# Local attention in a two-stage transformer kernel: exponentials transposed in 32x32 blocks on VectorE, mixing over 32 keys on four row groups, inverse norms on GpSimd

## The chip, the core and the metric

The kernel runs on one core of a Trainium2 chip. The metric is the device time of one execution in microseconds (us). Below, PE is TensorE (PEld its weight loads), DVE is VectorE, ACT is ScalarE, POOL is GpSimd, SP issues DMAs.

## The reference

The input is 16 sequences of 256 tokens of 128 numbers, all fp32. Three blocks run first (a linear attention, a mixture of experts, a causal attention with softmax feature maps), each with a residual and a layer norm. The fourth block has six layers, and the change lies in them. A layer, for each sequence:

```python
q, k, v = split(shift_tokens(x) @ Wqkv[i])      # 16 heads of 64
q = l2norm(q) * q_scale;  k = l2norm(k) * k_scale
q, k = rotary(q, scale), rotary(k, 1 / scale)
# windows of 32 queries; each sees its own 32 keys and the 32 before them
sim  = einsum('bhwie,bhwje->bhwij', q, k2) * 8.0   # 32 x 64 per window and head
attn = softmax(where(mask, -big, sim))
x = einsum('bhwij,bhwje->bhwie', attn, v2) @ Wo[i] + x
x = feed_forward(shift_tokens(x)) + x            # norm, 128 -> 2 x 341, gelu gate, 341 -> 128
```

A last layer norm ends the program.

## The kernel before, in words

Everything stays in fp32. The tokens of a unit (two sequences) lie in SBUF with the 128 features on the partitions (`xs`, with 32 zero columns ahead of a sequence). The program has two plans: one for the first three blocks, one for the six layers. A plan is a list of steps (`step(engine, work, function, after, takes, uses, rank, ...)`); `Plan.run` (line 87) walks them in a modelled time with the declared `work` of each in us, and on each engine issues the ready step of lowest rank whose buffers are free. The issued order is fixed when the program is built. Ranks are the number of the sequence tile plus entries of two tables, the dictionary passed to `Plan` (line 1013) and `due` (line 1028). Buffers come from `slots` (line 992): `pair` are the four PSUM tiles of 128x1024 (two banks each, all of PSUM), the others lie in SBUF.

A sequence is worked on in two tiles `t` of 128 tokens:

- `projections` (line 1059): queries and keys of 16 heads into a pair (PE, line 1071); the squares (ACT, line 1092) and their sums over a head (DVE, line 1098, into `ss`); the two halves of the rotation (DVE, lines 1078 and 1085), added on POOL (line 1095).
- `rotations` (line 1133): `norms` turns the 64 sums of a sequence into inverse norms by an integer first guess and three Newton steps (`inv_norm`, DVE, lines 1046 to 1057); POOL scales (line 1141), PE transposes (line 1145), ACT copies out (line 1151).
- `windows` (line 1180): for mixing, tokens must lie on the partitions, as a window's 64 keys, once in each half of 128 partitions. ACT spreads the tokens (line 1187), PE does 8 transposes (line 1196), ACT copies 1024 columns out (line 1202).
- `attention` (line 1213), for each tile: scores in four calls (PE, line 1228, 64 rows x 32 columns of the array, two heads and four windows side by side); mask and maximum (DVE, 1236, 1250); difference (POOL, 1253); exponential (ACT, 1257); sum and reciprocal (DVE, 1261, 1262); division (POOL, 1265). Then the exponentials `e` (queries on partitions) are turned by 8 transposes (PE, line 1269) and copied to `eT` (ACT, line 1310). Mixing (PE, line 1280) is two calls of four matmuls: for a window of 32 queries and one head of each two, 64 rows (keys) x 128 features, over 256 columns (8 heads x 32 queries). Each call fills one pair, and ACT copies it to `zT` (line 1289). Values are not projected: the product of the value and the output weights (`wvo`, made once a layer by `join`) is applied behind.
- `output` (line 1333): 16 accumulated matmuls over 256 tokens (PE, line 1340); added into `xs` (DVE, line 1349).
- `feed_forward` (line 1355) for each unit, with its gelu on ACT and its `root` on POOL (lines 1381 and 221).

A matmul of fp32 is recorded as two passes, a transpose as one.

Of the kernel before, what the change touches and what calls it, by code (L numbers as in the profile page):

```python
# [9 lines left out]
F32 = mybir.dt.float32  # L10
# [6 lines left out]
P = 128  # L17
NSEQ = 16
SEQ = 256
# [44 lines left out]
class Plan:  # L64
# [22 lines left out]
    def run(self):  # L87
# [15 lines left out]
        while left:  # L103
            moved = True
            while moved:
                moved = False
                for eng, heap in ready.items():
                    if at[eng] > now or not heap:
                        continue
                    back, got = [], None  # L110
                    while heap and len(back) < 64:
                        item = heapq.heappop(heap)
                        s = item[2]
                        if s.table and opened and s.table not in opened:
                            back.append(item)
                            continue
                        if s.count > 32 and self._dense(s, now, past, events):
                            back.append(item)
                            continue
                        kinds = [b.kind for b in s.takes]  # L120
                        if all(self._fits(kinds, k) for k in set(kinds)):
                            got = s
                            break
                        back.append(item)
                    for item in back:
                        heapq.heappush(heap, item)
# [66 lines left out]
def tile_kernel(ctx: ExitStack, tc: tile.TileContext, a: dict, out: bass.AP):  # L193
# [787 lines left out]
    with ExitStack() as st:  # L981
# [6 lines left out]
        def several(pl, n, shape, name):  # L988
# [4 lines left out]
            "pair": several(pp, 4, [P, 1024], "pp"),  # L993
            "kT": several(cd, 2, [P, 8, WIN + SEQ], "d_kT"),
            "qT": several(cd, 3, [P, 8, P], "d_qT"),
            "xw": several(cd, 2, [P, TPS * NB, P], "d_xw"),
            "sq": several(cd, 2, hs, "d_sq"),
            "t1": several(cd, 5, hs, "d_t1"),
            "ss": several(cd, 3, [P, 2, 2, HEADS, 2], "d_ss"),
            "t2": several(cd, 2, hs, "d_t2"),  # L1000
            "e": several(cd, 2, [P, 8, 2, 2 * WIN], "d_e"),
            "eT": several(cd, 2, [P, 8, P], "d_eT"),
            "zT": several(cd, 2, [P, SEQ // QB, HEADS, QB], "d_zT"),
            "xc": several(cd, 1, [P, TPU, P], "f_xc"),
# [5 lines left out]
        for ss in slots["ss"]:  # L1010

            pool.memset(ss, 1e-24)
        plan = Plan(slots, {
            "projections.product": -3,
            "feed_forward.turn": 1.5,
            "attention.mix": -1.5,
            "attention.divide": -0.5,
            "output.product": 2,
            "attention.below": 5,
            "projections.first": -0.5,  # L1020
            "projections.squares": 0.5,
            "projections.second": -1,
            "final.turn_back": -3,
            "windows.turn": -1,
            "rotations.norms": 3,
        })

        due = {
# [14 lines left out]
        magic = cd.tile([P, NN], I32, name="d_magic")  # L1043
        pool.memset(magic, 1597463007)

        def inv_norm(ss):

            x, y, t = (sd.tile([P, NN], F32, name=f"d_n{k}", bufs=2) for k in "xyt")
            dve.tensor_reduce(x, ss.rearrange("p t g h b -> p (t g h) b"), AX.X, ALU.max)
            dve.scalar_tensor_tensor(  # L1050
                y.bitcast(I32), x.bitcast(I32), -0.5, magic, ALU.mult, ALU.add
            )
            for _ in range(3):
                dve.scalar_tensor_tensor(t, y, 1.0, y, ALU.mult, ALU.mult)
                dve.scalar_tensor_tensor(t, t, -0.5, x, ALU.mult, ALU.mult)
                dve.scalar_tensor_tensor(y, t, 1.5, y, ALU.add, ALU.mult)  # L1056
            return y

        def projections(q, t):
# [35 lines left out]
                pool.tensor_tensor(t1.t, t1.t, t2.t, ALU.add)  # L1095

            def squares(qk, sq):
                dve.tensor_reduce(q.ss.t[:, t, qk, :, 0], sq.t, AX.X, ALU.add)  # L1098
# [34 lines left out]
        def rotations(q):  # L1133


            def norms():
                q.rn = inv_norm(q.ss.t)

            def scale(t, qk, t1):
                k = (2 * t + qk) * HEADS  # L1140
# [11 lines left out]
                    dst.t[:, :, off : off + P], pz.t.rearrange("p (c n) -> p c n", n=P)  # L1152
                )

            nm = step("dve", 4.4, norms, q.reds, [], [q.ss], q.rank + due["norms"])
            q.kT = Buf("kT")
            for t in range(TPS):
                turned(q, t, nm, scale, turn, put)
# [21 lines left out]
        def windows(q):  # L1180

            pz, rank = Buf("pair"), q.rank

            def spread():
                x = q.x
                src = bass.AP(x.tensor, x.offset, [x.ap[0], [WIN, TPS * NB], [0, 2], [1, 2 * WIN]])
                act.copy(
                    xd.t.rearrange("p h d -> p (h d)").rearrange(
                        "p (b a k) -> p b a k", a=2, k=2 * WIN
                    ),  # L1190
                    src,
                )

            def turn():
                for b in range(TPS * NB):
                    pe.transpose(
                        pz.t[:, b * P : (b + 1) * P],
                        xd.t.rearrange("p h d -> p (h d)")[:, b * P : (b + 1) * P], ident,
                    )

            def put():
                act.copy(q.xw.t.rearrange("p b d -> p (b d)"), pz.t)  # L1202

            xd, q.xw = Buf("sq"), Buf("xw")
            begun = every[q.n - 1].soft[0] if q.n else None
            dp = step("act", 0.96, spread, [*q.ready, begun], [xd, q.xw, pz], [], rank)
            tn = step("pe", 1.02, turn, [dp], [], [xd, pz], rank + due["windows"], count=16)
            q.spread = step(
                "act", 0.91,
                put, [tn], [], [pz, q.xw], rank,  # L1210
            )

        def attention(q, t):

# [49 lines left out]
            def divide():  # L1264
                pool.tensor_tensor(each(), each(), bc(o.z, es, 2), ALU.mult)  # L1265

            def turn(pz):
                for c in range(8):
                    pe.transpose(  # L1269
                        pz.t[:, c * P : (c + 1) * P],  # L1270
                        e.t[:, c, :, :].rearrange("p a k -> p (a k)"), ident,
                    )

            def mix(g, pz):

                for j in range(2):
                    b = 2 * g + j
                    for par in range(2):
                        r = slice(par * DH, (par + 1) * DH)
                        pe.matmul(  # L1280
                            pz.t[:, par * 512 : (par + 1) * 512].rearrange(
                                "p (c n) -> p c n", n=QB
                            )[:, :, j * WIN : (j + 1) * WIN],
                            lhsT=q.xw.t[r, t * NB + b, :],
                            rhs=eT.t[r, :, b * WIN : (b + 1) * WIN], start=True, stop=True,
                        )

            def put(g, pz):
                act.copy(q.zT.t[:, 2 * t + g, :, :].rearrange("p h n -> p (h n)"), pz.t)  # L1289

            sc = []
            for g in range(4):
# [14 lines left out]
            pz = Buf("pair")  # L1307

            def put_e():
                act.copy(eT.t.rearrange("p c n -> p (c n)"), pz.t)  # L1310

            te = step(
                "pe", 1.03, partial(turn, pz), [dv], [pz], [e], rank + due["turn"], count=16
            )
            pe_ = step(
                "act", 0.91,
                put_e, [te], [eT], [pz], rank,
            )
            if t == 0:
                q.zT = Buf("zT")  # L1320
            for g in range(2):
                pz2 = Buf("pair")
                new = [q.zT] if t == 0 and g == 0 else []
                mx = step(
                    "pe", 1.06, partial(mix, g, pz2), [pe_, q.spread, *q.mixed[:1]], [pz2, *new],
                    [eT, q.xw] + ([] if new else [q.zT]), rank + due["mix"], count=16,
                )
                q.mixed.append(mx)
                q.outs.append(
                    step("act", 0.91, partial(put, g, pz2), [mx], [], [pz2, q.zT], rank)  # L1330
                )

        def output(q):

            pr = Buf("pair")

            def product():

                for h in range(HEADS):
                    pe.matmul(  # L1340
                        pr.t[:, :SEQ], lhsT=q.w["vo"][:, h, :], rhs=q.zT.t[:, :, h, :],
                        start=(h == 0), stop=(h == HEADS - 1),
                    )
# [331 lines left out]
```

## Time and profile before

| | |
|---|---|
| median of 3 runs | 4375.44 us (4375.12 to 4377.77) |
| the profiled execution | 4371.72 us |
| its span, first to last instruction | 4369.9 us |
| mean granted PE clock | 0.989 |
| instructions | 106,120 |
| DMA | 37.13 MB, mean 8 GB/s |

The page gives for each engine its busy time, then a row of 40 slices of the span (a digit is the busy share in tenths, PEclk the clock that PE was granted), then groups of instructions: line, engine, operation, destination and sources by the program's names, shapes, count, then busy us and mean ns of one, then idle time ahead of them and who ended it. The end of a matmul is modelled, so that times of PE calls are read better from start to start.

### The profile page before, as it was taken

What the parts mean: (1) busy time and instruction counts of PE and PEld (TensorE: products, weight loads), DVE (VectorE), ACT (ScalarE), POOL (GpSimd) and SP (SyncE); (2) the same over time, 40 slices, a digit from 0 to 9 for tenths busy, and PEclk for the clock granted to TensorE, in tenths of its full rate; (3) what the DMA queues carried; (4) which work ended last, traced back from release to release, by engine and by line L of the source; (5) the groups of instructions that cost most, each with busy time, mean ns of one, the idle gap of its engine ahead of it and who ended that gap; (6) DMA issues with size and microseconds to landing.
All of it is one profiled execution on the core that took longest, in us unless ns stands there. A gap on an engine that the chain in (4) does not pass through costs nothing. (4 is left out here: it accounts for less than half of the span.)

```text
span 4369.9 us, 106120 instructions
## 1 busy us (share of the span) xinstructions
PE 4191.8 (96%) x45648; PEld 2978.9 (68%) x45648; DVE 3633.8 (83%) x6064; ACT 2674.8 (61%) x3514; POOL 2978.6 (68%) x1717
## 2 busy tenths in 40 slices
PE   8999999998699999999999999999999999999998
PEld 6777877877466666666666666666666666666666
DVE  6888888877788888878888888888888878888895
ACT  6766767664466566566656656666665665665654
POOL 2655545555787777767777778777777777777773
PEclk9999999999899999999999999999999999999999
DMA  3000000000000000000000000000000000000000
GB/s 88 4 6 6 3 4 1 4 3 3 20 2 11 2 13 2 7 11 2 13 2 6 11 2 13 2 7 11 2 12 2 7 11 2 2 2 6 6 14 18
DMA packets 30834, 37.13 MB, mean 8 GB/s; under 512 B 5407, under 2 KB 24349, under 8 KB 29597
## 3 DMA queue, kind: packets, MB, share of 16 engines
q1 hardware_dynamic: 30364, 30.35, 2.3%
q8 instruction: 359, 5.88, 0.6%
q14 instruction: 111, 0.90, 0.1%
HBM read 26.15 MB, written 4.19 MB: 7 GB/s over the span
## 5 line engine op out<-in xcount | busy, mean ns | idle before, releaser
L1095 POOL TENSOR_TENSOR d_t<-d_t,d_t 128x1024 f32<-128x1024 f32 x384 | 906.3, 2366 | 301.7 <-DVE d_t L1078 230.7
L1141 POOL TENSOR_TENSOR d_t<-d_t,d_ny 128x1024 f32<-128x1024 f32 x384 | 718.8, 1902 | 242.3 <-DVE d_ny L1056 242.3
L1071 PE MATMUL pp<-d_wqkv,xs 128*128 128x512 f32 x1536 | 736.7, 605 | 6.5 <-ACT d_sq L1092 1.6
L1340 PE MATMUL pp<-d_zT,d_wvo 128*128 128x256 f32 x3072 | 687.5, 382 | 1.2 <-DVE d_t L1078 0.5
L1340 PEld LDWEIGHTS pp<-d_zT,d_wvo 128*128 128x128 f32 x3072 | 575.9, 190 | 85.0 <-ACT d_xw L1202 1.3
L1092 ACT ACTIVATE d_sq<-pp 128x1024 f32<-128x1024 f32 x384 | 393.4, 1024 | 313.8 <-PE pp L1071 174.4
L1085 DVE TENSOR_TENSOR d_t<-pp,d_tab 128x1024 f32<-128x1024 f32 x384 | 466.3, 1215 | 135.4 <-ACT d_sq L1092 94.5
L1265 POOL TENSOR_TENSOR d_e<-d_e,d_z 128x1024 f32<-128x1024 f32 x192 | 363.5, 1902 | 229.6 <-DVE d_z L1262 228.3
L1289 ACT COPY d_zT<-pp 128x1024 f32<-128x1024 f32 x384 | 384.1, 1016 | 192.6 <-PE pp L1280 190.3
L1078 DVE TENSOR_TENSOR d_t<-pp,d_tab 128x1024 f32<-128x1024 f32 x384 | 463.7, 1209 | 19.0 <-ACT d_sq L1092 19.0
L1228 PEld LDWEIGHTS pp<-d_kT,d_qT 64*32 64x32 f32 x24576 | 230.2, 106 | 352.9 <-issue 202.1
L1098 DVE TENSOR_REDUCE d_ss<-d_sq 128x16 f32<-128x1024 f32 x384 | 463.3, 1209 | 0.1
L1280 PE MATMUL pp<-d_eT,d_xw 64*128 64x256 f32 x3072 | 425.9, 402 | 21.7 <-DVE d_t L1078 12.7
L1145 PE MATMUL pp<-ident,d_t 128*128 128x128 f32 x3072 | 404.2, 278 | 35.5 <-POOL d_t L1141 24.0
L1071 PEld LDWEIGHTS pp<-d_wqkv,xs 128*128 128x128 f32 x1536 | 271.4, 191 | 241.5 <-issue 217.2
L1145 PEld LDWEIGHTS pp<-ident,d_t 128*128 128x128 f32 x3072 | 344.8, 142 | 104.6 <-issue 56.4
L1257 ACT ACTIVATE d_e<-d_e 128x1024 f32<-128x1024 f32 x192 | 202.8, 1057 | 317.4 <-POOL d_e L1253 312.7
L1228 PE MATMUL pp<-d_kT,d_qT 64*32 64x64 f32 x24576 | 348.7, 223 | 28.7 <-DVE d_t L1078 25.0
L1253 POOL TENSOR_TENSOR d_e<-d_e,d_m 128x1024 f32<-128x1024 f32 x192 | 363.7, 1903 | 16.7 <-DVE d_m L1250 16.7
L848 POOL TENSOR_TENSOR c_e<-c_e,c_sm 128x1024 f32<-128x1024 f32 x128 | 248.7, 1950 | 178.2 <-DVE c_sm L844 121.8
L1280 PEld LDWEIGHTS pp<-d_eT,d_xw 64*128 64x128 f32 x3072 | 270.7, 187 | 104.0 <-ACT d_eT L1310 28.3
L835 POOL TENSOR_TENSOR c_e<-c_mn,c_e 128x512 f32<-128x512 f32 x128 | 139.7, 1091 | 196.3 <-ACT c_e L825 95.7
(187 smaller groups left out, 8083.1 us busy)
## 6 DMA issues: line engine op xcount, KB each, us to landing
d_wqkv<-L_ffn_Wqkv SPq DMA_DIRECT2D x6, 1024.0 KB
d_t<-L_ffn_Wqkv SPq DMA_DIRECT2D x10, 256.0 KB
d_t<-L_ffn_Wo SPq DMA_DIRECT2D x10, 256.0 KB, 3.0
a_xin<-L_attn_x SPq DMA_DIRECT2D x8, 256.0 KB, 2.9
keep<-bc_x SPq DMA_DIRECT2D x8, 256.0 KB, 2.0
d_t<-keep SPq DMA_DIRECT2D x8, 256.0 KB, 3.0
out<-d_t SPq DMA_DIRECT2D x8, 256.0 KB, 2.4
d_w<-L_ffn_W SPq DMA_DIRECT2D x6, 341.0 KB
```

The lines of the kernel that those rows point to most:

```text
L1071: pe.matmul(pj.t[:, hf * 512 : (hf + 1) * 512], lhsT=xj, rhs=q.w["qkv"][:, c : c + 512], start=True, stop=True,)
L1078: dve.tensor_tensor(t1.t, heads(pj.t), bc(q.lay.tab[:, 0, t, cc], hs, 1), ALU.mult)
L1085: dve.tensor_tensor(t2.t.rearrange("p h (x d) -> p h x d", x=2), swapped(pj.t), bc(q.lay.tab[:, 1, t, cc].rearrange("p (x d) -> p x d", x= ...
L1092: act.activation(sq.t, heads(pj.t), AF.Square)
L1095: pool.tensor_tensor(t1.t, t1.t, t2.t, ALU.add)
L1098: dve.tensor_reduce(q.ss.t[:, t, qk, :, 0], sq.t, AX.X, ALU.add)
L1141: pool.tensor_tensor(t1.t, t1.t, bc(q.rn[:, k : k + HEADS], hs, 2), ALU.mult)
L1145: pe.transpose(pz.t[:, c * P : (c + 1) * P], t1.t[:, 2 * c : 2 * c + 2, :].rearrange("p h d -> p (h d)"), ident,)
L1228: pe.matmul(pS.t[b * WIN : (b + 1) * WIN, s0 : s0 + 2 * WIN], lhsT=qT.t[r, c, b * WIN : (b + 1) * WIN], rhs=kT.t[r, c, k0 : k0 + 2 * WIN], ...
L1280: pe.matmul(pz.t[:, par * 512 : (par + 1) * 512].rearrange("p (c n) -> p c n", n=QB)[:, :, j * WIN : (j + 1) * WIN], lhsT=q.xw.t[r, t * NB ...
L1289: act.copy(q.zT.t[:, 2 * t + g, :, :].rearrange("p h n -> p (h n)"), pz.t)
L1340: pe.matmul(pr.t[:, :SEQ], lhsT=q.w["vo"][:, h, :], rhs=q.zT.t[:, :, h, :], start=(h == 0), stop=(h == HEADS - 1),)
```

## The change

It is in the plan's rule and in the layer stage.

1. The exponentials of a tile are transposed by one DVE instruction in blocks of 32x32 (keys by queries, within each 32 partitions) straight from `e` to `eT`. The 8 PE transposes and the ACT copy go.
2. Mixing takes 32 keys at a time: two halves `j` of the 64 keys accumulate in PSUM. A matmul has 32 rows (one block of keys, on the row group of its block of queries), 128 features, 512 columns (16 heads x 32 queries). One call per tile does all 8 and takes two pairs at once. `zT` has blocks of 32 queries.
3. `windows` transposes 128 tokens straight out of `xs`, at offsets of 0 and 32: four transposes, no spreading, 512 columns copied out.
4. `inv_norm` runs on POOL in 14 instructions over 128x64, with the lower bound as an operation of its own in place of an extra slot in `ss`.
5. Both tables of ranks change. In `Plan.run`, a step that needs two buffers of a kind and has only one free keeps that one from steps behind it.

```diff
                         kinds = [b.kind for b in s.takes]
-                        if all(self._fits(kinds, k) for k in set(kinds)):
+                        if all(self._fits(kinds, k) for k in set(kinds)) and not any(k in kept for k in kinds):
                             got = s
                             break
+                        if not kept:
+                            kept = [
+                                k for k in set(kinds)
+                                if kinds.count(k) > 1
+                                and all(self._fits(kinds, m) for m in set(kinds) - {k})
+                            ]
...
-            "xw": several(cd, 2, [P, TPS * NB, P], "d_xw"),
+            "xw": several(cd, 2, [P, 2 * TPS, P], "d_xw"),
-            "ss": several(cd, 3, [P, 2, 2, HEADS, 2], "d_ss"),
+            "ss": several(cd, 3, [P, TPS, 2, HEADS], "d_ss"),
-            "eT": several(cd, 2, [P, 8, P], "d_eT"),
-            "zT": several(cd, 2, [P, SEQ // QB, HEADS, QB], "d_zT"),
+            "eT": several(cd, 2, [P, 2, HEADS, WIN], "d_eT"),
+            "zT": several(cd, 2, [P, TPS * NB, HEADS, WIN], "d_zT"),
...
-            pool.memset(ss, 1e-24)
         plan = Plan(slots, {
-            "projections.product": -3,
+            "projections.product": -6,
...
+        def inv_norm(x):
+            y, t = (sd.tile([P, NN], F32, name=f"d_n{k}", bufs=3) for k in "yt")
+            pool.tensor_scalar(x, x, 1e-24, None, ALU.max)
+            pool.tensor_scalar(
+                y.bitcast(I32), x.bitcast(I32), -0.5, 1597463007.0, ALU.mult, ALU.add
             )
             for _ in range(3):
-                dve.scalar_tensor_tensor(t, y, 1.0, y, ALU.mult, ALU.mult)
-                dve.scalar_tensor_tensor(t, t, -0.5, x, ALU.mult, ALU.mult)
-                dve.scalar_tensor_tensor(y, t, 1.5, y, ALU.add, ALU.mult)
+                pool.tensor_tensor(t, y, y, ALU.mult)
+                pool.tensor_tensor(t, t, x, ALU.mult)
+                pool.tensor_scalar(t, t, -0.5, 1.5, ALU.mult, ALU.add)
+                pool.tensor_tensor(y, y, t, ALU.mult)
             return y
...
-            nm = step("dve", 4.4, norms, q.reds, [], [q.ss], q.rank + due["norms"])
+            nm = step("pool", 2.8, norms, q.reds, [], [q.ss], q.rank + due["norms"])
...
             def turn():
-                for b in range(TPS * NB):
-                    pe.transpose(
-                        pz.t[:, b * P : (b + 1) * P],
-                        xd.t.rearrange("p h d -> p (h d)")[:, b * P : (b + 1) * P], ident,
-                    )
+                for t in range(TPS):
+                    for j in range(2):
+                        n = 2 * t + j
+                        c = t * P + j * WIN
+                        pe.transpose(pz.t[:, n * P : (n + 1) * P], q.x[:, c : c + P], ident)
             def put():
-                act.copy(q.xw.t.rearrange("p b d -> p (b d)"), pz.t)
+                act.copy(q.xw.t.rearrange("p b d -> p (b d)"), pz.t[:, : 2 * TPS * P])
...
-            dp = step("act", 0.96, spread, [*q.ready, begun], [xd, q.xw, pz], [], rank)
-            tn = step("pe", 1.02, turn, [dp], [], [xd, pz], rank + due["windows"], count=16)
+            tn = step("pe", 0.5, turn, [*q.ready, begun], [pz, q.xw], [], rank + due["windows"], count=8)
...
-            def turn(pz):
-                for c in range(8):
-                    pe.transpose(
-                        pz.t[:, c * P : (c + 1) * P],
-                        e.t[:, c, :, :].rearrange("p a k -> p (a k)"), ident,
-                    )
+            def turn():
+                dve.transpose(
+                    eT.t,
+                    e.t.rearrange("p c a (j k) -> p j (c a) k", j=2),
+                )
-            def mix(g, pz):
+            def mix(ps):
                 for j in range(2):
-                    b = 2 * g + j
-                    for par in range(2):
-                        r = slice(par * DH, (par + 1) * DH)
+                    for b in range(NB):
+                        r = slice(b * WIN, (b + 1) * WIN)
                         pe.matmul(
-                            pz.t[:, par * 512 : (par + 1) * 512].rearrange(
-                                "p (c n) -> p c n", n=QB
-                            )[:, :, j * WIN : (j + 1) * WIN],
-                            lhsT=q.xw.t[r, t * NB + b, :],
-                            rhs=eT.t[r, :, b * WIN : (b + 1) * WIN], start=True, stop=True,
+                            ps[b // 2].t[:, (b % 2) * 512 : (b % 2 + 1) * 512],
+                            lhsT=q.xw.t[r, 2 * t + j, :],
+                            rhs=eT.t[r, j, :, :].rearrange("p h n -> p (h n)"),
+                            start=(j == 0), stop=(j == 1),
                         )
...
+            te = step("dve", 1.15, turn, [dv], [eT], [e], rank + due["turn"])
+            ps = [Buf("pair"), Buf("pair")]
+            new = [] if q.mixed else [q.zT]
+            mx = step(
+                "pe", 2.1, partial(mix, ps), [te, q.spread, *q.mixed], [*ps, *new],
+                [eT, q.xw] + ([] if new else [q.zT]), rank + due["mix"], count=32,
+            )
...
-                        pr.t[:, :SEQ], lhsT=q.w["vo"][:, h, :], rhs=q.zT.t[:, :, h, :],
-                        start=(h == 0), stop=(h == HEADS - 1),
+                        pr.t[:, :SEQ], lhsT=q.w["vo"][:, (h % 2) * 8 + h // 2, :],
+                        rhs=q.zT.t[:, :, h, :], start=(h == 0), stop=(h == HEADS - 1),
```

More of the change, by code (lines that the diff above doesn't have):

```diff
@@ L109, in run @@
                         continue
-                    back, got = [], None
+                    back, got, kept = [], None, ()
                     while heap and len(back) < 64:
@@ L1009, in tile_kernel @@
             pool.memset(kT[:, :, 0:WIN], 0.0)
-        for ss in slots["ss"]:
-            pool.memset(ss, 1e-24)
         plan = Plan(slots, {
-            "projections.product": -3,
+            "projections.product": -6,
             "feed_forward.turn": 1.5,
             "attention.mix": -1.5,
-            "attention.divide": -0.5,
-            "output.product": 2,
+            "attention.divide": -1.5,
+            "output.product": 4,
             "attention.below": 5,
-            "projections.first": -0.5,
+            "projections.first": -4.5,
             "projections.squares": 0.5,
             "projections.second": -1,
-            "final.turn_back": -3,
+            "final.turn_back": -2,
             "windows.turn": -1,
             "rotations.norms": 3,
+            "attention.top": 3,
+            "attention.mask": 2,
+            "projections.rotated": 4,
+            "join.turn": 0.5,
+            "attention.turn": 4,
+            "attention.exps": 1.5,
+            "feed_forward.turn_back": -2,
+            "attention.total": 1.5,
+            "feed_forward.inner": 3,
         })
@@ L1042, in tile_kernel @@
         NN = TPS * 2 * HEADS
[L1043 to L1051, printed above, removed]
+        def inv_norm(x):
[3 more added lines that the diff above has]
+                y.bitcast(I32), x.bitcast(I32), -0.5, 1597463007.0, ALU.mult, ALU.add
             )
             for _ in range(3):
-                dve.scalar_tensor_tensor(t, y, 1.0, y, ALU.mult, ALU.mult)
-                dve.scalar_tensor_tensor(t, t, -0.5, x, ALU.mult, ALU.mult)
-                dve.scalar_tensor_tensor(y, t, 1.5, y, ALU.add, ALU.mult)
+                pool.tensor_tensor(t, y, y, ALU.mult)
+                pool.tensor_tensor(t, t, x, ALU.mult)
+                pool.tensor_scalar(t, t, -0.5, 1.5, ALU.mult, ALU.add)
+                pool.tensor_tensor(y, y, t, ALU.mult)
             return y
@@ L1097, in squares @@
             def squares(qk, sq):
-                dve.tensor_reduce(q.ss.t[:, t, qk, :, 0], sq.t, AX.X, ALU.add)
+                dve.tensor_reduce(q.ss.t[:, t, qk, :], sq.t, AX.X, ALU.add)
             for qk in range(2):
@@ L1136, in norms @@
             def norms():
-                q.rn = inv_norm(q.ss.t)
+                q.rn = inv_norm(q.ss.t.rearrange("p t g h -> p (t g h)"))
             def scale(t, qk, t1):
@@ L1182, in windows @@
             pz, rank = Buf("pair"), q.rank
[L1184 to L1191, printed above, removed]
-                )
-            def turn():
-                for b in range(TPS * NB):
-                    pe.transpose(
-                        pz.t[:, b * P : (b + 1) * P],
-                        xd.t.rearrange("p h d -> p (h d)")[:, b * P : (b + 1) * P], ident,
-                    )
+            q.xw = Buf("xw")
+            def turn():
+                for t in range(TPS):
[3 more added lines that the diff above has]
+                        pe.transpose(pz.t[:, n * P : (n + 1) * P], q.x[:, c : c + P], ident)
             def put():
-                act.copy(q.xw.t.rearrange("p b d -> p (b d)"), pz.t)
-            xd, q.xw = Buf("sq"), Buf("xw")
+                act.copy(q.xw.t.rearrange("p b d -> p (b d)"), pz.t[:, : 2 * TPS * P])
             begun = every[q.n - 1].soft[0] if q.n else None
-            dp = step("act", 0.96, spread, [*q.ready, begun], [xd, q.xw, pz], [], rank)
-            tn = step("pe", 1.02, turn, [dp], [], [xd, pz], rank + due["windows"], count=16)
[L1208 to L1211, printed above, removed]
+            tn = step("pe", 0.5, turn, [*q.ready, begun], [pz, q.xw], [], rank + due["windows"], count=8)
+            q.spread = step("act", 0.6, put, [tn], [], [pz, q.xw], rank)
         def attention(q, t):
@@ L1265, in divide @@
                 pool.tensor_tensor(each(), each(), bc(o.z, es, 2), ALU.mult)
-            def turn(pz):
-                for c in range(8):
-                    pe.transpose(
-                        pz.t[:, c * P : (c + 1) * P],
-                        e.t[:, c, :, :].rearrange("p a k -> p (a k)"), ident,
-                    )
-            def mix(g, pz):
+            def turn():
[4 more added lines that the diff above has]
+            def mix(ps):
                 for j in range(2):
-                    b = 2 * g + j
-                    for par in range(2):
-                        r = slice(par * DH, (par + 1) * DH)
+                    for b in range(NB):
+                        r = slice(b * WIN, (b + 1) * WIN)
                         pe.matmul(
-                            pz.t[:, par * 512 : (par + 1) * 512].rearrange(
-                                "p (c n) -> p c n", n=QB
-                            )[:, :, j * WIN : (j + 1) * WIN],
-                            lhsT=q.xw.t[r, t * NB + b, :],
-                            rhs=eT.t[r, :, b * WIN : (b + 1) * WIN], start=True, stop=True,
+                            ps[b // 2].t[:, (b % 2) * 512 : (b % 2 + 1) * 512],
+                            lhsT=q.xw.t[r, 2 * t + j, :],
+                            rhs=eT.t[r, j, :, :].rearrange("p h n -> p (h n)"),
+                            start=(j == 0), stop=(j == 1),
                         )
             def put(g, pz):
-                act.copy(q.zT.t[:, 2 * t + g, :, :].rearrange("p h n -> p (h n)"), pz.t)
+                b = t * NB + 2 * g
+                act.copy(q.zT.t[:, b : b + 2, :, :].rearrange("p b h n -> p (b h n)"), pz.t)
             sc = []
@@ L1306, in attention @@
             dv = step("pool", 1.87, divide, [sm], [], [e], rank)
[L1307 to L1318, printed above, removed]
+            te = step("dve", 1.15, turn, [dv], [eT], [e], rank + due["turn"])
             if t == 0:
                 q.zT = Buf("zT")
-            for g in range(2):
[L1322 to L1328, printed above, removed]
+            ps = [Buf("pair"), Buf("pair")]
[4 more added lines that the diff above has]
+            )
+            q.mixed.append(mx)
+            for g in range(2):
                 q.outs.append(
-                    step("act", 0.91, partial(put, g, pz2), [mx], [], [pz2, q.zT], rank)
+                    step("act", 0.91, partial(put, g, ps[g]), [mx], [], [ps[g], q.zT], rank)
                 )
```

## The prediction, made before the changed kernel was run

> **What bounds the kernel now.** I read the page's first two parts first, for the engine that is never free and for the clock it was granted.
>
> ```profile
> PE 4191.8 (96%) x45648; PEld 2978.9 (68%) x45648; DVE 3633.8 (83%) x6064; ACT 2674.8 (61%) x3514; POOL 2978.6 (68%) x1717
> PE   8999999998699999999999999999999999999998
> PEclk9999999999899999999999999999999999999999
> ```
>
> TensorE (PE) is full except in slices 10 and 11, where the first plan ends and the layer plan begins. The first projection of the layer plan starts at 1091.8 us and the last output product at 4338.8 us; the change touches only this stage. So I took a steady part of it, 1600 to 3600 us, and asked for the engines' busy time and for the same of the output product (line 1340) alone.
>
> ```profile
> 1600.00:3600.00 2000.00, 1971.98 (x24505) 1335.48 (x24502) 1702.86 (x2495) 1235.63 (x1287) 1511.34 (x792) 1.00 0.02 7
> 1600.00:3600.00 2000.00, 430.03 (x1920) 359.86 (x1920) 1.00 0.02 7
> ```
>
> The first row lists PE, weight loads, DVE, ACT, POOL, then the clock. A sequence has 32 instructions of line 1340, so 1920 are 60 sequences: **one in 33.33 us**, 96 of them in 3200 us. Per sequence PE is busy 32.87 (98.6%), DVE 28.38, ACT 20.59, POOL 25.19. All PE waits that are put down to another engine there come to some 28 us in 2000. A shorter PE list shortens the kernel, until DVE or POOL is full.
>
> Then the timeline of PE, for what one call really takes: from its start to the start of what follows, because the modelled ends overlap.
>
> ```profile
> 2422.09 1.14 PE L1280 MATMUL pp<-d_eT,d_xw 64*128 64x256 f32 x8
> 2423.15 0.45 PE L1228 MATMUL pp<-d_kT,d_qT 64*32 64x64 f32 x32
> 2423.53 1.13 PE L1280 MATMUL pp<-d_eT,d_xw 64*128 64x256 f32 x8
> 2424.60 0.45 PE L1228 MATMUL pp<-d_kT,d_qT 64*32 64x64 f32 x32
> 2424.98 1.09 PE L1269 MATMUL pp<-ident,d_e 128*128 128x128 f32 x8
> 2426.01 0.45 PE L1228 MATMUL pp<-d_kT,d_qT 64*32 64x64 f32 x32
> ```
>
> A mixing call takes 1.06 us, a turn of the exponentials 1.03 before scores (0.87 where another transpose or projection follows), a call of scores 0.38.
>
> **The change on PE.**
> - The turn of the exponentials goes: two per sequence at 0.87 to 1.03, I take 0.95, **-1.90 us**.
> - The window turn (line 1196) has 4 transposes in place of 8; eight took 0.87 from start to start (2462.69 to 2463.56, busy 1.04): **-0.47** (bounds 0.43 and 0.52).
> - The mixing. Before, a call has 4 matmuls of 64 rows x 256 columns, each recorded as two passes. The single records of the first call above show a pair of passes, one for each row group, start 7 ns apart, and pairs start at 2422.086, .406, .622 and .838: a pass of 256 columns is 0.216 us and two row groups run together. Of 1.06 us, 4 x 0.216 = 0.864 are passes, some 0.2 are first weights and the end. The new call has 8 matmuls of 32 rows x 512 columns; a 512-column pass is 0.43 (projections, line 1071: 1.81 us for 4). If four row groups run together each has 2 keys' halves x 2 passes = 4 x 0.43 = 1.73, with 0.2 around it 1.93. Two calls are 3.86 in place of 4 x 1.06 = 4.25: **-0.39**. No row shows 32-row groups. Bounds: all four together (-0.39), and one at a time (2 x (16 x 0.43 + 0.2) = 14.2, so +9.9). I take the first, because the nearest row, the scores, runs 32 passes of 64 columns in 0.38 us on 2 x 4 tiles: 32 x 54 ns (a quarter of 0.216 us) in line would be 1.7 us.
>
> PE: 32.87 - 1.90 - 0.47 - 0.39 = **30.1 us a sequence**.
>
> **On DVE.** I read its groups and POOL's.
>
> ```profile
> L1050 DVE SCALAR_TENSOR_TENSOR d_ny<-d_nx,d_magic 128x64 int32<-128x64 int32 x60 | 60.9, 1015 | 2.1
> L1261 DVE TENSOR_REDUCE d_z<-d_e 128x16 f32<-128x1024 f32 x120 | 144.5, 1204 | 4.6 <-ACT d_e L1257 3.8
> L1095 POOL TENSOR_TENSOR d_t<-d_t,d_t 128x1024 f32<-128x1024 f32 x240 | 566.7, 2367 | 179.3 <-DVE d_t L1078 137.9 <-PE pp L1071 26.8 <-DVE d_t L1085 14.5
> L1381 POOL TENSOR_SCALAR f_rs<-f_mv 128x4 f32<-128x4 f32 x30 | 7.0, 232 | 0.0
> L1463 POOL TENSOR_TENSOR d_tab<-d_rope,d_sc 128x256 f32<-128x256 f32 x8 | 5.6, 727 | 0.0
> ```
>
> The norms leave DVE: 0.29 (line 1049) + 1.02 (line 1050) + 2.06 (123.4 us of lines 1054 to 1056 over 60) = -3.36. Two 32x32 block transposes of 128x1024 come. No row shows one. Every DVE operation over 1024 elements takes 1.20 to 1.22; bounds 1.13 (their start-to-start) and 2.42 (two passes). I take 1.21, +2.42. DVE: 28.38 - 3.36 + 2.42 = **27.4**, at the upper price 29.9; both below PE. The wait it adds: the transpose stands in DVE's queue for POOL's division, with projections' products behind it that free PSUM and feed POOL. The plan orders it late; POOL's line 1265 already waits on DVE 2.5 us a sequence.
>
> The Trainium skill ("VectorE: DVE Perf Modes", The three transpose paths) has 311 ns for a 128x128 bf16 DVE transpose and says that it only works inside 32x32 blocks, which is all that is wanted here. By it, as an estimate, eight of them would be 2.5 us, and the DVE sum 30.0; no run so far shows it.
>
> **On POOL.** The norms arrive as 14 dependent instructions of 128x64: 9 with two tensors, 5 with one. Rows: 0.232 at 128x4 with one tensor, 0.727 at 128x256 and 2.367 at 128x1024 with two; the line through the last two gives 0.32 at 64. So 9 x 0.32 + 5 x 0.25 = 4.1, and with 0.09 between dependent instructions (line 1381 to line 221, 2446.50 to 2446.59) 5.3. The step's declared work in the diff is 2.8, and other declared works agree with the trace (1.87 for line 1141 back to back). Bounds 14 x 0.154 = 2.2 (a 128x66 fill) and 14 x 0.727 = 10.2. I take 4.0, nearest the row of 0.232 and the line. POOL: 25.19 + 4.0 = **29.2**. What stands behind them is the scaling (line 1141), which already waits 2.5 us a sequence for the norms, so part of the new work falls into that wait. The initial fill of the sums' tiles, three instructions once, is nothing.
>
> A rule speaks against this move: the skill ("GPSIMD Engine Reference", opening) calls this engine the wrong choice for ordinary elementwise arithmetic, VectorE being about 2x faster. The rows agree on the ratio: 2.367 (line 1095) against 1.21 (line 1078). By the rule the norms would stay on DVE, and its sum would be 28.38 + 2.42 = 30.8, above PE's 30.1: here the slower engine has the room.
>
> **On ACT** two copies of 1.02 a sequence (line 1310) go, and the spreading copy of 1.06 (line 1187), and the window copy is halved: about -3.5 of 20.6, not a bound. The chain exponentials to mixing loses a step (PE turn and ACT copy become one DVE step); it wasn't what PE waited for.
>
> **The order.** The ranks and the rule that keeps a freed tile for a step that needs two re-order everything; I cost them at nothing beside idle time. PE idles 0.46 us a sequence now, with DVE at 85% and POOL at 76%. After, DVE is at 88% and POOL at 94%, and a mixing call takes two of four PSUM pairs at once. I take 1.0 us of idle: a period of **31.1 us**. No code before 1091 us changes its work.
>
> **Sum.** (33.33 - 31.1) x 96 = 214 us off the profiled execution's 4371.72 us (span 4369.9): 4158. The median of the runs is 3.7 us above that execution, so about **4160**.
>
> **Rivals.**
> 1. *PE stays as full as now* (0.20). For: ACT and DVE are lighter, POOL's norms may cost the declared 2.8. Period 30.1/0.986 = 30.5; 2.8 x 96 = 270; 4105.
> 2. *POOL becomes the bound* (0.17). For: its slack is the smallest and the norms' price the least known. At 6.5 us POOL holds 31.7, at 98% 32.3: 4276. Against: it idles 8.1 us a sequence now, 2.5 of them for these very norms.
> 3. *PSUM pairs* (0.10). Mixing needs two pairs together. A call used a pair for 2.2 us (2422.09 to the end of the copy at 2424.28); now two are held 3.4 and 4.4. If PE waits 0.8 us for the second pair at each of two calls, the period is 32.7 with the idle time above: 4315; half of it 4238.
> 4. *Slower: the 32-row groups don't run four at a time* (0.06). Two at a time a call is 8 x 0.43 + 0.2 = 3.65, two are 7.3, PE is 33.5, the period 34.0: 4440; one at a time PE is 40.4 and the time 5110. It decides from about 2.2 groups at once, where the two calls eat the 2.4 us that the turns give back.
> 5. *The change does not do what it says* (0.02): the new order leaves PE idle for all that it is relieved of, 4375.
>
> The forecast has 0.45. The range from 4085 to 4300 holds it, most of rivals 1 and 2 and half of 3. About 0.2% (9 us) is what a measurement can tell from no change; faster by more 0.92, within it 0.02, slower 0.06.
>
> **What would show it.** Right: line 1269's transposes gone, mixing calls of about 1.95 us with four passes starting within some 20 ns, line 1340 once in 31 us, PE at 96 to 97% in the steady part. A DVE transpose well over 1.25 us, norms over 5 us on POOL, or PE waiting for the copies out of the mixing's pairs would show rivals at work. It is wrong if the mixing's passes start one after another, or if PE's idle time grows by over 2 us a sequence.

## The result, and the profile after

The changed kernel takes 4450.2 us (median of 4 runs, 4446.8 to 4450.9) against 4375.7 before: a ratio of 1.0168, interval 1.015 to 1.0185. It is **slower by 1.7%**, where 5% faster was forecast. The profiled execution took 4446.82 us, its span 4445.0.

From the page of the changed kernel, the busy line and the rows of PE and of its clock:

```profile
PE 4085.7 (92%) x43728; PEld 2676.3 (60%) x43728; DVE 3517.9 (79%) x5200; ACT 2329.6 (52%) x3226; POOL 3367.4 (76%) x3057
PE   8999999998788999998999999999999999999998
PEclk9999999999899999999999999999999999999999
```

PE has less to do, and so have DVE and ACT; only POOL has more. Yet nothing is full: PE is at 92% of a longer span. The same steady stretch as before, first all engines, then the output product (now line 1325):

```profile
1600.00:3600.00 2000.00, 1850.99 (x22746) 1115.33 (x22745) 1601.44 (x1899) 982.54 (x1068) 1710.15 (x1597) 0.99 0.03 7
1600.00:3600.00 2000.00, 420.31 (x1888) 353.98 (x1888) 0.99 0.03 7
```

1888 / 32 = 59 sequences in 2000 us: one in 33.90 us, where it was 33.33. Per sequence PE is busy 31.37 and idle 2.53 (before: 32.87 and 0.47), DVE busy 27.14, ACT 16.65, POOL 28.99. The new operations in that stretch (line, engine, shapes, count, then busy us, mean ns of one, idle ahead of them):

```profile
L1277 PE MATMUL pp<-d_eT,d_xw 32*128 32x512 f32 x1888 | 276.0, 627 | 36.8 <-ACT d_zT L1286 30.9 <-DVE d_t L1090 5.8
L1267 DVE STREAM_TRANSPOSE d_eT<-d_e 128x1024 f32<-128x1024 f32 x118 | 146.3, 1240 | 38.9 <-POOL d_e L1263 38.0
L1066 POOL TENSOR_TENSOR d_nt<-d_nt,d_ss 128x64 f32<-128x64 f32 x177 | 56.5, 319 | 13.8
L1067 POOL TENSOR_SCALAR d_nt<-d_nt 128x64 f32<-128x64 f32 x177 | 43.0, 243 | 15.5
```

The transpose costs 1.24 us. Mixing itself does what was forecast where nothing interrupts it: the single records of the call at 2402.14 show four passes start at 2402.144, .151, .157 and .164, one on each row group, the next fours at 2402.678, 2403.107 and 2403.536, and the next operation at 2404.07, so 1.93 us. But it is not always left alone. A stretch of PE's timeline (in brackets idle time, and who ended it):

```profile
2423.78 2.00 PE L1277 MATMUL pp<-d_eT,d_xw 32*128 32x512 f32 x16
2425.71 1.17 PE L1226 MATMUL pp<-d_kT,d_qT 64*32 64x64 f32 x96
2427.09 1.13 PE L1277 MATMUL pp<-d_eT,d_xw 32*128 32x512 f32 x4 [0.21 <-DVE d_t L1090]
2429.03 1.99 PE L1277 MATMUL pp<-d_eT,d_xw 32*128 32x512 f32 x12 [0.82 <-ACT d_zT L1286]
```

The second call has run 4 of its 16 passes, the ones of its first pair, and stops: its second pair is still being copied out by ACT. ACT's timeline in the same stretch:

```profile
2427.02 1.06 ACT L1255 ACTIVATE d_e<-d_e 128x1024 f32<-128x1024 f32 x1 [2.45 <-POOL d_e L1251]
2427.98 1.91 ACT L1286 COPY d_zT<-pp 128x1024 f32<-128x1024 f32 x2
2430.24 1.93 ACT L1286 COPY d_zT<-pp 128x1024 f32<-128x1024 f32 x2 [0.34 <-PE pp L1277]
```

The copies of the first call, whose last passes started at about 2425.2, stand in ACT's queue behind an exponential, and that waited 2.45 us for POOL's difference (line 1251). POOL's timeline says why (first and last instruction of the norms, then the difference):

```profile
2419.92 0.38 POOL L1060 TENSOR_SCALAR d_ss<-d_ss 128x64 f32<-128x64 f32 x1
...
2424.81 0.32 POOL L1068 TENSOR_TENSOR d_ny<-d_ny,d_nt 128x64 f32<-128x64 f32 x1
2425.09 1.90 POOL L1251 TENSOR_TENSOR d_e<-d_e,d_m 128x1024 f32<-128x1024 f32 x1
```

The norms take 5.17 us, 2419.92 to 2425.09, and the difference stands behind them; its own input (the maximum, line 1248 on DVE) had been there since about 2420.7. Of the 59 norms in the stretch, 30 have the difference directly behind them and 29 the feed-forward's root. The step that issues the norms declares 2.8 us, and the plan placed what follows by that; whether this length is what costs the time is for the experiments to show.

### The profile page after: what moved, and what is told of

Its sections match the earlier page's. It is cut to its first block, busy times and chain, and to the rows that moved or that the text cites. A ratio compares the mean times of both kernels' runs of the same rounds, so it can differ in the third digit from the quotient of the medians.

```text
span 4445.0 us, 101898 instructions
## 1 busy us (share of the span) xinstructions
PE 4085.7 (92%) x43728; PEld 2676.3 (60%) x43728; DVE 3517.9 (79%) x5200; ACT 2329.6 (52%) x3226; POOL 3367.4 (76%) x3057
## 5 line engine op out<-in xcount | busy, mean ns | idle before, releaser
L1083 PE MATMUL pp<-d_wqkv,xs 128*128 128x512 f32 x1536 | 749.6, 613 | 72.7 <-ACT d_kT L1163 40.0
L1277 PE MATMUL pp<-d_eT,d_xw 32*128 32x512 f32 x3072 | 452.7, 628 | 57.1 <-ACT d_zT L1286 37.5
L1157 PE MATMUL pp<-ident,d_t 128*128 128x128 f32 x3072 | 418.9, 283 | 45.1 <-POOL d_t L1153 36.1
L1226 PEld LDWEIGHTS pp<-d_kT,d_qT 64*32 64x32 f32 x24576 | 242.5, 106 | 342.1 <-issue 238.8
L1286 ACT COPY d_zT<-pp 128x1024 f32<-128x1024 f32 x384 | 369.2, 1012 | 140.6 <-PE pp L1277 119.0
L1386 PE MATMUL pp<-f_xn,d_w 128*128 128x512 f32 (+1 forms) x576 | 317.0, 638 | 59.2 <-DVE d_t L1090 50.1
L1226 PE MATMUL pp<-d_kT,d_qT 64*32 64x64 f32 x24576 | 335.0, 224 | 3.8 <-ACT d_kT L1163 2.5
L1277 PEld LDWEIGHTS pp<-d_eT,d_xw 32*128 32x128 f32 x3072 | 159.5, 186 | 246.1 <-issue 100.7
```

The source lines that it names most:

```text
L1083: pe.matmul(pj.t[:, hf * 512 : (hf + 1) * 512], lhsT=xj, rhs=q.w["qkv"][:, c : c + 512], start=True, stop=True,)
L1157: pe.transpose(pz.t[:, c * P : (c + 1) * P], t1.t[:, 2 * c : 2 * c + 2, :].rearrange("p h d -> p (h d)"), ident,)
L1226: pe.matmul(pS.t[b * WIN : (b + 1) * WIN, s0 : s0 + 2 * WIN], lhsT=qT.t[r, c, b * WIN : (b + 1) * WIN], rhs=kT.t[r, c, k0 : k0 + 2 * WIN], ...
L1277: pe.matmul(ps[b // 2].t[:, (b % 2) * 512 : (b % 2 + 1) * 512], lhsT=q.xw.t[r, 2 * t + j, :], rhs=eT.t[r, j, :, :].rearrange("p h n -> p ( ...
L1286: act.copy(q.zT.t[:, b : b + 2, :, :].rearrange("p b h n -> p (b h n)"), pz.t)
```

## The experiments

Theory A at the start: the norms' time over the declared one stands in a chain of queues that sets the period. Rivals: B, the two PSUM pairs and the new order make the idle time whatever the norms take; C, POOL is simply full. All times are medians; ratios are to the kernel before, measured beside each. The period is read from the output product in the stretch from 1600 to 3600 us, as above.

| run | us | ratio (interval) | period us |
|---|---|---|---|
| change, 1 Newton step | 4243.7 | 0.9697 (0.9682 to 0.9711) | 31.7 |
| change, 2 steps | 4305.8 | 0.9839 (0.9824 to 0.9854) | 32.8 |
| change (3 steps) | 4450.2 | 1.0168 (1.015 to 1.0185) | 33.9 |
| change, 5 steps | 4825.4 | 1.1026 (1.1004 to 1.1048) | 38.5 |
| change, norms on DVE | 4553.1 | 1.0404 (1.0387 to 1.0421) | 35.1 |
| before, norms on POOL | 4630.4 | 1.0581 (1.0565 to 1.0596) | 36.4 |
| change, norms declared 5.2 | 4567.3 | 1.0435 (1.0419 to 1.045) | 35.7 |
| change, other ranks | 4320.3 | 0.9868 (0.9852 to 0.9885) | 32.4 |
| other ranks, 1 step | 4302.1 | 0.9822 (0.9806 to 0.9839) | 32.3 |
| other ranks, 5 steps | 4604.2 | 1.0514 (1.0493 to 1.0535) | 35.7 |
| 2 steps, ranks of their own | 4286.5 | 0.9796 (0.9781 to 0.981) | 32.3 |
| norms on DVE, ranks of their own | 4386.8 | 1.0017 (1.0008 to 1.0027) | 33.3 |

**The norms' length, in the issued order of the change.** One line differs, with 1, 2 or 5 in place of 3; the traces have the same order of operations on PE, DVE, ACT and POOL:

```diff
-            for _ in range(3):
+            for _ in range(1):
                 pool.tensor_tensor(t, y, y, ALU.mult)
```

> The changed kernel with one Newton step in place of three in the inverse norms (the other two are left out, so the norms are less exact); the issued order stays the same, because the declared work stays 2.8. Norms on POOL take about 0.46 + 0.32 + 4 x 0.375 = 2.3 us in place of the 5.2 that the changed kernel's timeline shows. Theory A (the order was made for 2.8 us, and the 2.4 us above that stand in a chain of POOL and DVE steps that now sets the period): the period falls from 33.9 to about 31.5 to 32, the time to 4220 to 4280. Theory B (the two PSUM pairs that a mixing call takes at once, and the new order itself, make the idle time): the time stays within 20 us of 4450. Theory C (POOL is simply full): it is at 29.0 us busy and 1.1 of gaps of 33.9, so that nothing changes either.

> The changed kernel with five Newton steps in place of three (two more are computed than needed), order unchanged. Norms take 5.2 + 8 x 0.375 = 8.2 us. Theory A: each us more is a us of the period: 3.0 x 96 = 288 us, 4740. Theory B: POOL has 3.8 us of room in the period, and the time stays within 40 us of 4450. Theory C: POOL's sum becomes 33.1, still under 33.9: up to 4480.

> The changed kernel with two Newton steps in place of three (the third is left out, the norms are a little less exact), order unchanged. Norms take 0.46 + 0.32 + 8 x 0.375 = 3.8 us. The runs with one, three and five steps gave 4244, 4450 and 4825. Theory A (the norms' time stands in the chain that sets the period, from some point on): on or under the straight line between one and three steps, 4300 to 4350. If the excess sets in only over the declared 2.8 us it lies nearer to 4244. Theory B (idle time from the PSUM pairs) has no place for a change: 4450.

4244, 4306 and 4825: B and C both fall. In the traces the norms take 2.17 us with one step, from their first instruction to the difference, and 3.66 with two. So with 3.0 us less (the expectation had 2.9) the time drops by 206 us, more than the whole loss. The first half of these 3.0 us costs 62 us and the second 144, which fits an excess that sets in somewhere above the declared 2.8 us; no run has norms of just that length. With 3.0 us more it is 375, over the 288 foretold; the granted clock of that run is also lower, 0.943 (0.982 in the change, 0.988 with one step). How the waits grow with the norms is seen in PE's waits in the steady stretch (us in total, times, longest). One step, the whole answer:

```profile
PE pp L1386 <- DVE d_t L1090: 40.1, 62, 1.1
PE pp L1202 <- DVE d_t L1090: 19.2, 31, 0.7
PE pp L1202 <- DVE d_e L1234: 16.0, 27, 0.6
PE pp L1277 <- DVE d_t L1090: 5.9, 27, 0.6
```

Three steps, the change as it was, the whole answer:

```profile
PE pp L1386 <- DVE d_t L1090: 38.3, 58, 1.1
PE pp L1277 <- ACT d_zT L1286: 30.9, 29, 2.8
PE pp L1083 <- ACT d_kT L1163: 29.0, 26, 1.1
PE pp L1202 <- DVE d_t L1090: 25.8, 29, 3.4
PE pp L1083 <- ACT d_zT L1286: 19.2, 26, 0.7
PE pp L1277 <- DVE d_t L1090: 5.8, 26, 0.6
```

Two and five steps, the line of mixing that waits for the copies:

```profile
PE pp L1277 <- ACT d_zT L1286: 5.5, 4, 1.6
```

```profile
PE pp L1277 <- ACT d_zT L1286: 104.9, 26, 5.8
```

The three lines in which PE waits for ACT are not there with one step. They don't hold all of the stop, because the modelled end of a matmul hides part of it as busy time: the four passes at 2427.09 above count 1.13 us, and one call of the one-step run is recorded as busy throughout and takes 2.86 us from its start to the next operation's:

```profile
2408.00 2.93 PE L1277 MATMUL pp<-d_eT,d_xw 32*128 32x512 f32 x16
2410.86 1.10 PE L1157 MATMUL pp<-ident,d_t 128*128 128x128 f32 x8
```

So the calls are better taken from start to start. Over 1.93 us each, the mixing calls of the stretch lose 4 us in all with one step (125 calls, 4 of them stopped), 24 with two, 71 with three (118 calls, 33 of them over by more than 0.1 us) and 224 with five (104 calls). From one step to three that is 1.15 us a sequence; the projections' waits for ACT (line 1083) add 0.82; together they are 2.0 of the 2.15 us by which the period grows. What ACT itself waits for, first in the change and then with one step:

```profile
ACT d_e L1255 <- POOL d_e L1251: 222.8, 88, 11.7
```

```profile
ACT d_e L1255 <- POOL d_e L1251: 97.5, 36, 8.7
```

This is the chain of the timelines above, from POOL through ACT's queue to PE. PSUM has its part in it, as the place where PE is stopped, but in this order hardly before the copies are late.

**The parts one by one.** The norms back on DVE within the change (only the line of its step is shown; `inv_norm` goes back to DVE with it, in 11 instructions), and the norms alone moved in the kernel before:

```diff
-            nm = step("pool", 2.8, norms, q.reds, [], [q.ss], q.rank + due["norms"])
+            nm = step("dve", 4.4, norms, q.reds, [], [q.ss], q.rank + due["norms"])
```

> The changed kernel with the norms on DVE, as before the change (11 instructions, declared 4.4); the ranks are those of the changed kernel, the plan orders anew. Theory A: the gain of the turns and of mixing comes back in part, with DVE at 27.1 + 3.4 + 0.4 = 30.9 us: a period of 32 to 33.5, 4290 to 4400. Theory B: 4450 within 30 us, since mixing still takes two pairs at once.

> The kernel before with only the norms on POOL, as in the change (14 instructions, declared 2.8), with the ranks and the mixing of before. Theory A: this part alone costs: PE holds 32.9 us a sequence already and the late norms come on top of the chain: a period of 34 to 35, 4440 to 4540. Theory B: within 20 us of 4376 or faster, since DVE is relieved of 3.4 us and POOL has room at 25.2 + 5.2 = 30.4 of 33.3.

Both are slower than either theory allowed: 4553 and 4630. In the first no engine is full (of 2000 us, PE 1831, DVE 1716, POOL 1435). A part can't be priced by taking it out under the ranks of another kernel: each plan orders anew, and the new order has a price of its own. For the first that is shown below (ranks of its own bring it to 4387); the second had no run with other ranks, so how much of its loss is the order stays open. In the second, what PE waits for most are the copies out of mixing's pairs again, here ahead of the transposes of the exponentials (line 1264), though a mixing call there still takes one pair at a time:

```profile
PE pp L1264 <- ACT d_zT L1284: 56.9, 24, 2.4
```

ACT waits 381 us there for POOL's difference (196 in the kernel before, where PE has no such wait for the copies). So PE can come to wait for these copies without a call that takes two pairs at once. Both results made the order itself the suspect, apart from the price that was declared.

**The declaration alone, and another order.** The first changes one number. The second keeps every operation of the change, declares the works close to what they measured (norms, mixing, transpose), and has other ranks throughout, chosen in the plan's own arithmetic with those works.

```diff
-            nm = step("pool", 2.8, norms, q.reds, [], [q.ss], q.rank + due["norms"])
+            nm = step("pool", 5.2, norms, q.reds, [], [q.ss], q.rank + due["norms"])
```

The second has this besides:

```diff
-            "projections.product": -6,
...
-            "output.product": 4,
...
-            "projections.first": -4.5,
...
-            "projections.rotated": 4,
...
+            "projections.product": -50.0,
...
+            "output.product": 56.0,
...
+            "projections.first": -36.5,
...
+            "projections.rotated": 34.0,
...
```

> The changed kernel with three steps, the norms declared at the 5.2 us that they take in place of 2.8; operations and ranks as in the change, the plan orders anew. Theory A1 (the false declaration is the fault): at least half of the excess over the one-step run goes, 4350 or less. Theory A2 (these ranks make an order in which the norms stand in the chain, whatever is declared): 4420 to 4500.

> Every operation of the changed kernel, three steps and all, with the works declared as measured (norms 5.2, mixing 1.95, transpose 1.17) and other ranks throughout, chosen so that the next sequence's projections run ahead and the norms have slack before the scaling needs them. Theory A2 (the order is at fault, the operations are not): the period falls to 32 to 33, 4270 to 4350, faster than before the change (4376). Rival B (a mixing call that takes two PSUM pairs, or norms on POOL, cost this in any order): 4420 or more.

> Two Newton steps (one left out), declared at 3.75, mixing and transpose declared as measured, ranks chosen anew for that. Theory A2: PE is left with 30.1 to 30.5 us of work in a period of 31.3 to 31.8: 4200 to 4260. Rival B: no better than the same kernel in its first order (two steps, 4300 to 4450).

The right declaration under the old ranks is worse still: 4567. What PE waits for there is another thing, the first line of its waits:

```profile
PE pp L1277 <- DVE d_eT L1267: 44.5, 17, 5.2
```

Theory A1 falls: the true length, declared under the old ranks, makes another order, and a worse one. With other ranks the same operations take **4320, faster than before by 1.3%** (0.9852 to 0.9885), and 130 us less than the change as it was. All engines, then the output product (line 1350 there) in the steady stretch:

```profile
1600.00:3600.00 2000.00, 1918.19 (x23748) 1193.06 (x23726) 1675.60 (x1994) 1051.00 (x1118) 1787.06 (x1671) 0.99 0.02 7
1600.00:3600.00 2000.00, 436.44 (x1976) 371.82 (x1977) 0.99 0.02 7
```

61.75 sequences, 32.4 us each; PE is idle 1.3 us of that, close to the 1.0 of the forecast, but its busy time is 31.1 where 30.1 was forecast. Its mixing calls lose 67 us in the stretch from start to start, and still 67 us with one Newton step (below), so that this loss does not hang on the norms. The two-step run with ranks of its own missed its expectation (4286 for 4200 to 4260), though it beats the first order by 19 us.

**Are the norms out of the chain there?** The same edits of the Newton steps, now in the other order, and the norms on DVE with ranks found in the same way:

> The run with other ranks (4320, three steps) with one Newton step (two are left out), its order unchanged: the same 2.9 us that were worth 206 us in the order of the change. Theory A2 (in this order the norms have slack and stand in no chain): 4270 to 4325, less than a quarter of 206. Rival (norms cost their time in any order): 4115.

> The run with other ranks (4320, three steps) with five Newton steps (two more than needed), order unchanged: the same 3.0 us that cost 375 us in the order of the change. POOL then holds 28.9 + 1.1 of gaps + 3.0 = 33.0 us a sequence, which is over the 32.4 of the period, so that some loss is certain. Theory A2: the slack takes a part, 4400 to 4620. Rival (norms cost their time in any order): 4695.

> The run with the norms on DVE (4553 with the ranks of the change) with ranks chosen anew for it and the works declared as measured (norms 3.9, mixing 1.95, transpose 1.17). Theory A2 (the order is at fault, not the operations): 4320 to 4390, since DVE holds 30.1 us and POOL 25.2 a sequence. Its rival (norms on DVE can't be hidden with the transposes there): 4480 or more.

The 3.0 us that were worth 206 us in the order of the change are worth 18 here (4302). Three more cost 284, against 375; there POOL's sum of 33.0 exceeds the old period, as foretold. With the norms on DVE and an order made for that the change is level with the kernel before (4387, 1.0008 to 1.0027): so between the two orders made for their operations the move to POOL is worth 66 us, and the rest of the change without it gains nothing. Neither order is known to be the best, and the other ranks are not better throughout: with one Newton step the order of the change is the faster by 58 us (4244 against 4302).

## Why the prediction was wrong

- *PE's floor, 30.1 us a sequence: right to 0.4 us.* In the one-step run, whose PE was granted the full clock in the steady stretch, PE is busy 1918.69 / 63 = 30.46. (In the changed kernel itself it is 31.37, for the reason below.) The mixing call was given 1.93 and takes 1.93; four row groups do run together, so rival 4 has no part in the slower time.
- *DVE, 27.4: right* (27.14; the transpose 1.24 for 1.21). The estimate worked out from the Trainium skill ("VectorE: DVE Perf Modes", The three transpose paths), eight times 311 ns for 128x128 in bf16, would have made 2.5 us of one instruction over 1024 columns; the trace has half of that, and it decides. ACT fell by 3.9 instead of 3.5.
- *The norms' price: wrong by my choice.* The working gave 5.3, and they take 5.17. I took 4.0, because the declared 2.8 pulled the value down. That a declared work agrees with the trace elsewhere said nothing of a step that had not run. POOL's busy sum (28.99 for 29.2) hides the error: of the 5.17 us, 4.13 count as busy, and the gaps between dependent instructions, 1.04 us, don't, but POOL ran nothing else in them.
- ***"The order ... I cost them at nothing beside idle time", with 1.0 us of idle: this is the step that failed.*** The period missed by 2.8 us (33.90 for 31.1): PE idles 2.53 us, 1.53 over the forecast, and is busy 31.37, 1.27 over it. Of the 0.9 us by which that exceeds the one-step run, 0.67 stand in the mixing line (4.68 us a sequence against 4.00), whose stopped calls count as busy. An order written for 2.8 us holds a queue for 5.17, and what stands behind it on POOL, then on ACT, is late. The sum of each engine's work said nothing of it: POOL has 3.9 us of the period free, and the period still falls by 2.15 us when the norms get 3.0 us shorter. The line "POOL at 94%" was a warning about throughput; the harm was in what stood behind the norms. The prediction named only the scaling there (line 1141, now 1153). The path behind the scaling may have a share, in the 29.0 us in which projections wait for the copy of the keys. It did not name the difference and, through ACT, the copies out of PSUM, nor the feed-forward's root, for which DVE waits 35.1 us in the stretch and not at all with one step.
- *Its own signs.* Norms over 5 us, PE waiting for the copies out of the mixing's pairs, and idle time that grows by over 2 us a sequence (2.06) all came; it had named them as signs of rivals at work or of being wrong. One reading was off, without effect on the sum: at 1091.8 us stands a semaphore event of the layer plan's first projection, whose first matmul starts at 1093.5.
- *The rivals.* PSUM pairs (3) described the place where PE stops, and POOL (2) the engine that holds it; neither gave a time above the one before, since both were priced as sums. The one slower rival was the wrong mechanism. Rival 5 came nearest, a new order that leaves PE idle, but it had a chance of 0.02 and ended at the time before. The chance of 0.06 for slower had no case in it for an order that does not fit.

What stays open: which single wait closes the loop. The trace shows a whole chain (norms, difference, exponential, copies, mixing) and that its last wait grows with the norms; no run exchanged two steps of one queue alone, so the shares of the difference, the scaling and the root are not told apart. That 4320 is the best order for these operations isn't shown either.

## What to carry to other kernels

In a kernel whose queues were ordered from declared durations, moving a step to another engine prices two things: its work on that engine, and every instruction that stands behind it in that queue if the declared time is short. Look at the declared work first, work it out from rows, and where it is too small, follow the queue: what waits behind it, whom that feeds, and whether PE's buffers hang on it. Putting the declared time right is not enough by itself: with the old ranks it gave 4567, and only an order with slack before the step's readers brought 4320. To test the operations of a change apart from its order, shorten the suspected step under the same order and give the same operations another order; the two runs here (4244 and 4320) said more than taking parts out. And where PE's ends are modelled, take a call from start to start: part of a stop counts as busy.

## What the runs showed of the hardware

A transpose of 128x1024 fp32 in 32x32 blocks takes DVE 1.24 us, nearly the 1.20 to 1.22 of its other operations of that size. On POOL, 128x64 takes 0.29 to 0.32 us with two tensors and 0.24 with one (the first of a chain 0.37), with about 0.08 us between dependent ones. Four row groups of 32 rows run fp32 passes of 512 columns together, their starts 7 ns apart; the last rounds of the call at 2402.14 are 0.43 us apart. The mean granted clock went from 0.989 (before, PE 96% busy) to 0.943 (five steps, 90%), but PE's busy share alone doesn't give it: it was 0.982 in the change and 0.962 with the norms declared 5.2, both at 92%, and 0.979 with the other ranks at 94%.
